# Layer 2 of a graph network's edge pipeline: features on partitions with 256 edges streaming, in place of edges on partitions

## The chip, the cores and the metric

The kernel runs on one core of a Trainium2 chip, as one program that computes the whole layer. The metric is the device time of one execution in microseconds (us), smaller being better. Durations inside an execution come from the hardware profiler. In what follows PE is TensorE (its matmuls; PEld are its weight loads), ACT is ScalarE, DVE is VectorE, POOL is GpSimd and SP is SyncE; a q behind a name (ACTq, SPq) is that engine's own instruction queue, where it issues DMAs and waits.

## The reference

There are 12500 nodes with 64 features each, and 200000 edges, sorted by their target `dst`. Each edge has 64 features of its own and a distance. With `ssp(v) = softplus(v) - log 2`, the reference computes

```python
nodes    = x[[src, dst]]                         # 128 numbers per edge
gates    = ssp(edge @ We1 + be1) @ We2 + be2     # 64 per edge
gates    = gates * (1 - sigmoid(5 * (distance - 3.5)))
h        = ssp(nodes @ Wn1 + bn1) @ Wn2 + bn2    # 64 per edge
message_sum = zeros.at[dst].add(h * gates)       # summed into the target node
new      = x + ssp(message_sum @ Ws1 + bs1) @ Ws2 + bs2
out      = layernorm(x + new)
```

All of it is float32.

## The kernel before

**Preparation.** The first 75 us load constants and compute a table, one row per node, of what a target node adds to the first layer. The additive constant of softplus is moved into the biases; each bias row is split into three bf16 pieces, so that a matmul of three rows can add it.

**The loop over edges.** The edges are taken in 391 groups of 512 (four lanes `k` of 128). Step `i` of the loop works on several groups at once: it loads for `i + 5`, gathers for `i + 14`, does the first layer of group `i + 1`, the second layer of group `i` and the sum into nodes of an earlier group. The order on every engine is the order in which the program writes the instructions.

- `gather` (L231): POOL issues an indirect DMA per lane, 128 rows of x by `src`. 47 of the 1564 lanes are fetched row by row instead, by plain DMAs on the queues of SP and ACT (`fetch`, L257: seven a step on SP, nine on ACT, with `read_rows`, L245, reading their addresses from a list). 1516 gathers are left for POOL. There are 19 buffers of gathered rows.
- `load` (L278, L286): SP brings the edges' features and the table's rows that the group's targets need.
- `transposes` (L307, or L304 for a lane fetched row by row): four transposes turn the gathered rows, with a one-hot of the target's place in a window of 42 nodes beside them, to features on partitions. They wait for the loads, the gathers and the one-hots of the group. `xcopy` (L314) on ACT copies the result to SBUF.
- First layer, with features on partitions: `layer1_bias` (L319), `layer1_edge` (L324) and `layer1_node` (L330) put 768 columns into PSUM tile `z` (two banks). `exps` (L341) and `logs` (L344) on ACT and `softplus` (L349) on DVE make `s` of them.
- Second layer, with edges on partitions: the activations are the stationary operand and the weights stream. `layer2_bias` (L354) adds both biases by a matmul of three rows, `layer2_edge` (L361) and `layer2_node` (L366) bring gates and h of the four lanes into one bank, tile `gh`, in two and four matmuls. On DVE `hcut` (L375) multiplies h by the cutoff and `message` (L379) multiplies that by the gates.
- `scatter` (L383): matmuls of the message with the one-hots sum the 512 messages into a window of 42 nodes, in the columns of the second bank of `z` that the first layer leaves free. `window` (L400) adds this to the sums in SBUF. It is done two groups behind (`i - 2`), and in the last steps, from `i = last - CLOSE` = 378 on, one group behind.

**Node blocks.** As soon as a block of 512 nodes has all its messages, its own two layers and its normalisation are cut into parts (`node_block`, L402 to L483) which are put into the following steps, after the step's own work: matmuls (L419, L447, L450), ACT work (L438, L439, L458, L466, L467), DVE work (the rest), a fetch and a store by SP. There are 25 blocks; the last is done when the loop is over. After the loop the last two groups are written out by hand.

A matmul of float32 is shown as two records, a transpose as one.

Of the kernel before, what the change touches and what calls it, by code (L numbers as in the profile page):

```python
# [57 lines left out]
P = 128  # L58
# [65 lines left out]
def gnn_resnorm_kernel(ctx: ExitStack, tc: tile.TileContext, a: dict, out: bass.AP, E: int):  # L124
# [56 lines left out]
    ones3 = const.tile([PIECES, HE], BF16, name="ones3")  # L181
    be3 = const.tile([PIECES, 2, D], BF16, name="be3")
    row3 = const.tile([PIECES, 2, K, D], BF16, name="row3")
    rs3 = const.tile([PIECES, K, D], BF16, name="rs3")
    wns = const.tile([DW, REST, 2, 2 * D], F32, name="wns")

# [100 lines left out]
                wns[D:DW, g % REST, h, :].bitcast(U8),  # L287
                table_bytes[:, bass.ds(bases[g][h], 8 * D * W)].rearrange("o (w f) -> (o w) f", w=W))), old)

    xTs, zs, us, ss, ghs, hs, msgs, scs = ({} for _ in range(8))  # L290

    def onehot(g):
        last = nc.vector.tensor_tensor(xgs[g][:, :, D:DW], iota, rel[:, g, :].to_broadcast([P, K, W]), OP.is_equal)  # L293
# [69 lines left out]
    def layer2_node(g):  # L363
        for h in range(2):
            for t in range(2):
                nc.tensor.matmul(ghs[g][:, 1, 2 * t + h, :], ss[g][:, 1 + h, t, :], wn2, start=False,  # L366
                                 stop=h == 1 and t == 1, skip_group_check=True)

    def layer2(g):
        layer2_edge(g)  # L370
        layer2_node(g)

    def hcut(g):
        hs[g] = work.tile([P, K, D], F32, name="h")
# [6 lines left out]
    def scatter(g, sc):  # L381
        for t in range(2):
            ins = nc.tensor.matmul(sc, msgs[g][:, 2 * t : 2 * t + 2, :].rearrange("p h f -> p (h f)"),  # L383
                                   xgs[g][:, 2 * t : 2 * t + 2, D:DW], start=t == 0, stop=t == 1, skip_group_check=True)
        note(("scatter", g), ins)
        scs[g] = sc
# [103 lines left out]
    with tc.manual_schedule():  # L490
# [4 lines left out]
        with tc.tile_pool(name="prep", bufs=1) as prep:  # L495
# [81 lines left out]
                    nc.vector.tensor_sub(rest, rest, pieces[:, q, :])  # L577
            nc.scalar.dma_start(row_d.rearrange("(o q) f -> o q f", o=1), pieces)
            rows = prep.tile([PIECES, 4, D], BF16, name="rows")
            nc.scalar.dma_start(rows.rearrange("q i d -> q (i d)"), row_d)  # L580
            for i in range(3, PARTS):
                load_x(i)
# [3 lines left out]
            for i in range(PARTS):  # L586
                for c in range(i * CP, (i + 1) * CP, CP // 2):
                    m = CP // 2
                    ps = z_tile().rearrange("p b (k f) -> p (b k) f", k=K)
                    for k in range(m):  # L590
                        nc.tensor.matmul(ps[:, k, :], xT[:, c + k, :], wnb, start=True, stop=True)
                    tb = prep.tile([P, m, 2 * D], F32, name="tb", bufs=6)
                    nc.scalar.copy(tb[:, :K, :], ps[:, :K, :])
                    nc.vector.tensor_copy(tb[:, K:, :], ps[:, K:m, :])
                    nc.sync.dma_start(by_node[:, c : c + m], tb)
                    nc.vector.memset(sums[:, c * P : WIDE if c + m == NCH else (c + m) * P], 0.0)
                if i == 1:
                    nc.vector.tensor_copy(base_i[:1], base_b[:1])
                    nc.vector.tensor_scalar(base_i[32:33], base_b[32:33], float(8 * D), None, OP.mult)
                    nc.vector.tensor_scalar(rows_i, rows_i, float(4 * D), None, OP.mult)  # L600
                    for k in range(2):
                        nc.vector.tensor_copy(be3[:, k, :], rows[:, 0, :])
                    for k in range(K):
                        nc.vector.tensor_copy(row3[:, :, k, :], rows[:, 1:3, :])
                        nc.vector.tensor_copy(rs3[:, k, :], rows[:, 3, :])
                if i == 2:
                    nc.scalar.activation(dist, dist, AF.Sigmoid, bias=steep, scale=-5.0)
                    nc.scalar.preload_act_table_set("natural_log_exp_and_others")
                    nc.vector.tensor_copy(rel, dst_i)
                    for t in range(2):  # L610
                        r = rel[:, :, 2 * t : 2 * t + 2]
                        nc.vector.tensor_sub(r, r, base_b[:, :NH].rearrange("p (g h) -> p g h", h=2))


        with tc.tile_pool(name="finish", bufs=1) as finish:
            blocks = list(zip(node_blocks(N), block_steps(N, NG)))
            last = NG - 1
            parts, begun, complete, rest = {}, None, 0, []

            def at(f, g, *more):  # L620
                if 0 <= g < NG:
                    f(g, *more)

            def behind_by(i):
                close = last - CLOSE
                return [g for g in ([i - 2] if i <= close else []) + ([i - 1] if i >= close else []) if g >= 0]

            for g in range(LOADS - 1):
                load(g)
            for g in range(2):  # L630
                onehot(g)
            for i in range(-1, last - 1):
                now = parts.pop(i, [])
                early = [part for part in now if part.tensor]
                at(load, i + LOADS)
                read_rows(i, 0, ROWS[0])
                fetch(i, 0, ROWS[0])
                if i >= 0:
                    at(gather, i + AHEAD)
                transposes(i + 1, ("load", i + 1), ("gather", i + 1), ("onehot", i + 1))  # L640
                xcopy(i + 1)
                read_rows(i, 1, ROWS[1])
                fetch(i, 1, ROWS[1] - 6)
                layer1_bias(i + 1)
                at(layer2_bias, i)
                for n, g in enumerate(behind_by(i)):
                    scatter(g, zs[i + 1][:, 1, HE + 2 * n * W : HE + 2 * (n + 1) * W])
                layer1_edge(i + 1)
                layer1_node(i + 1)
                exps(i + 1)  # L650
                fetch(i, 1, 3)
                logs(i + 1)
                fetch(i, 1, 3)
                for g in behind_by(i):
                    window(g)
                at(layer2, i)
                for part in early:
                    part.tensor(tx_tile())
                at(hcut, i)
                at(message, i)  # L660
                softplus(i + 1)
                for part in early:
                    part.others()
                at(onehot, i + 3)
                for part in now:
                    if not part.tensor:
                        part.others()
                complete = i
                if blocks and complete >= blocks[0][1] - PREPARE and not begun:
                    begun = node_block(*blocks[0][0], finish)  # L670
                    begun.pop(0).others()
                if blocks and complete >= blocks[0][1]:
                    steps = next(steps for steps in BLOCK_STEPS if i + steps[-1] < last - 1)
                    for n, part in zip(steps, begun):
                        parts.setdefault(i + n, []).append(part)
                    rest = begun[len(steps) :]
                    blocks.pop(0)
                    begun = None
            assert len(blocks) == 1 and begun and not parts


            begun.pop(2).others()
            transposes(last, ("load", last), ("gather", last), ("onehot", last))
            xcopy(last)
            layer1_bias(last)
            layer2_bias(last - 1)
            scatter(last - 2, zs[last][:, 1, HE : HE + 2 * W])
            layer1_edge(last)
            layer1_node(last)
            for some in (edge, node):  # L690
                exps(last, some)
                logs(last, some)
            square, variance, root, scale, store = (part.others for part in rest)
            square()
            window(last - 2)
            for g in range(last - 1, last + 1):
                window_bases(g)
            layer2(last - 1)
            layer2_bias(last)
            softplus(last, edge)  # L700
            layer2_edge(last)
            softplus(last, node)
            layer2_node(last)
            hcut(last - 1)
            message(last - 1)
            scatter(last - 1, tx_tile()[:, : 2 * W])
            variance()
            root()
            hcut(last)
            message(last)  # L710
            scatter(last, tx_tile()[:, : 2 * W])
            window(last - 1)
            window(last)
            hidden, clamp = begun.pop(0)
            hidden(gh_tile())
            scale()
            clamp()
            store()
            for part in begun:
                node_part(part)  # L720
# [152 lines left out]
```

## Time and profile before

| | us |
|---|---|
| median of 10 runs (1935.36 to 1939.39) | 1937.62 |
| the profiled execution, its own time | 1937.49 |
| its span, first to last instruction | 1935.6 |
| POOL busy (1516 gathers) | 1441.2 |
| PE busy | 1781.5 |
| ACT busy | 963.3 |
| DVE busy | 1053.1 |
| granted TensorE clock, mean | 0.972 |

Busy time is the sum of the instructions' durations with overlaps counted once. The ends of matmuls are modelled, so that distances between starts say more of PE than durations do. Groups of instructions are listed by line, engine and tile as `busy, mean ns of one | idle time of the engine just before them`, with what ended that idle time. In the order of time, a row has its start, its duration, engine, line and operation, how many instructions were merged into it, and in brackets the idle time before it. The waits list who waited for whom: total us, times, longest.

### The profile page before, as it was taken

The page shows a single profiled execution, that of the slowest core. Times are in us where ns is not written, and L with a number is a line of the kernel's source. Part 1 is how long each engine was busy: PE and PEld are TensorE (multiplying, and loading weights), DVE is VectorE, ACT ScalarE, POOL GpSimd, SP SyncE. Part 2 cuts the span into 40 slices and gives each one's busy share as a digit, 9 for nine tenths or more (in the row PEclk, how much of TensorE's full clock was granted, in tenths as well). Part 3 has the DMA queues.
Part 4 walks back from the last instruction along what each step waited for, and adds up shares of the span by engine and source line. Part 5 has one row for each costly group of instructions (what it writes and reads, how often), then busy time and mean ns, then how long its engine had stood idle before and what let it go on. Part 6 is the DMA issues. An engine that isn't in the chain of part 4 may idle for free.

```text
span 1935.6 us, 47845 instructions
## 1 busy us (share of the span) xinstructions
PE 1781.5 (92%) x11373; PEld 1463.4 (76%) x11373; DVE 1053.1 (54%) x2767; ACT 963.3 (50%) x1318; POOL 1441.4 (74%) x1520
## 2 busy tenths in 40 slices
PE   4899998999999999999999989999999999898997
PEld 4777777777777777777777777777777777787875
DVE  4455554554564554555555555555555555555565
ACT  1355554544554554545555555454555555555453
POOL 7777777777777777777777777777777777777773
PEclk9999999999998999999999999999999999999898
DMA  8422222222222222222222222222222222222220
GB/s 247 132 70 66 66 65 72 65 67 66 73 65 68 67 71 70 66 70 65 72 70 69 71 68 70 74 69 71 67 73 74 70 71 69 70 73 70 66 73 25
DMA packets 150911, 143.53 MB, mean 74 GB/s; under 512 B 51887, under 2 KB 98395, under 8 KB 150626
## 3 DMA queue, kind: packets, MB, share of 16 engines
q1 hardware_dynamic: 94090, 88.26, 15.7%
q0 software_dynamic: 48512, 49.77, 11.4%
q10 hardware_dynamic: 8024, 2.37, 0.6%
q8 instruction: 97, 1.59, 0.3%
q14 instruction: 188, 1.54, 0.3%
HBM read 130.59 MB, written 9.63 MB: 72 GB/s over the span
## 4 chain that ended last, share of the span: by engine, by line
PE 48%; ACTq 16%; issue 9%; SPq 9%; DMA 7%; ACT 6%; DVE 3%; POOL 2%; DVEq 0%; POOLq 0%
ACTq L257 13%; PE z L330 10%; PE gh L366 7%; PE z L383 7%; PE tx L307 6%; PE z L324 5%; PE gh L361 4%; SPq L257 4%; ACT xT L314 3%; DMA xg<-in_x,src_i 3%; PE gh L354 2%; DMA wns<-table 2%; PE z L319 2%; ACTq L245 2%; SPq L286 2%
## 5 line engine op out<-in xcount | busy, mean ns | idle before, releaser
L231 POOL DMA_INDIRECT xg<-in_x,src_i x1516 | 1441.2, 951 | 465.1 <-issue 346.9
L341 ACT ACTIVATE u<-z 128x768 f32<-128x768 f32 x392 | 317.0, 809 | 691.9 <-PE z L330 651.1
L400 DVE TENSOR_TENSOR sums<-sums,z 64x42 f32 x778 | 152.8, 196 | 771.9 <-ACT u L341 740.9
L330 PE MATMUL z<-xT,wns 106*128 106x256 f32 x1564 | 428.5, 398 | 8.0 <-ACT xT L314 7.2
L344 ACT ACTIVATE u<-u,one 128x768 f32<-128x768 f32 x392 | 366.0, 934 | 70.2 <-ACT u L341 66.1
L366 PE MATMUL gh<-consts,s 128*128 128x64 f32 x3128 | 399.0, 271 | 0.0
L366 PEld LDWEIGHTS gh<-consts,s 128*128 128x128 f32 x3128 | 389.1, 196 | 0.0
L349 DVE SCALAR_TENSOR_TENSOR s<-u,z 128x768 f32<-128x768 f32 x392 | 369.6, 943 | 12.5 <-ACT u L344 9.9
L330 PEld LDWEIGHTS z<-xT,wns 106*128 106x128 f32 x1564 | 299.7, 197 | 77.2 <-ACT xT L314 32.7
L307 PE MATMUL tx<-consts,xg 128*106 128x128 f32 x1517 | 237.0, 276 | 95.1 <-DMA wns<-table 33.0
L383 PEld LDWEIGHTS z<-xg,msg 128*128 128x128 f32 x1556 | 205.9, 193 | 125.8 <-issue 122.5
L314 ACT COPY xT<-tx 106x512 f32<-106x512 f32 x391 | 227.7, 582 | 132.2 <-PE tx L307 114.2
L383 PE MATMUL z<-xg,msg 128*128 128x84 f32 x1556 | 266.2, 294 | 0.7 <-DVE msg L379 0.2
L361 PEld LDWEIGHTS gh<-consts,s 128*128 128x128 f32 x1564 | 246.6, 199 | 24.6 <-DVE s L349 2.0
L324 PE MATMUL z<-eT,consts 128*128 128x256 f32 x782 | 255.5, 409 | 0.0
L307 PEld LDWEIGHTS tx<-consts,xg 128*106 128x106 f32 x1517 | 168.8, 139 | 112.3 <-issue 52.3
L361 PE MATMUL gh<-consts,s 128*128 128x128 f32 x1564 | 246.9, 281 | 1.7 <-DVE s L349 1.7
L375 DVE TENSOR_TENSOR h<-gh,cut 128x256 f32<-128x256 f32 x391 | 166.0, 425 | 31.4 <-PE gh L366 17.4
L379 DVE TENSOR_TENSOR msg<-gh,h 128x256 f32<-128x256 f32 x391 | 166.0, 424 | 13.4
L354 PE MATMUL gh<-row,ones 3*128 3x512 bf16 x391 | 147.6, 378 | 0.0
L293 DVE TENSOR_TENSOR xg<-consts,rel 128x168 f32<-128x168 f32 x391 | 128.4, 329 | 0.0
L324 PEld LDWEIGHTS z<-eT,consts 128*128 128x128 f32 x782 | 121.7, 197 | 0.9 <-issue 0.9
(93 smaller groups left out, 587.5 us busy)
## 6 DMA issues: line engine op xcount, KB each, us to landing
xr<-in_x ACTq DMA_DIRECT2D x3328, 0.2 KB
eT<-in_eT SPq DMA_DIRECT2D x195, 256.0 KB
xr<-in_x SPq DMA_DIRECT2D x2688, 0.2 KB
xg<-in_x,src_i POOLq DMA_INDIRECT x1516
wns<-table SPq DMA_DIRECT2D x782, 21.0 KB
table<-tb SPq DMA_DIRECT2D x14, 448.0 KB
sums<-in_xT SPq DMA_DIRECT2D x7, 455.0 KB
y<-in_x SPq DMA_DIRECT2D x24, 128.0 KB
```

Of the source, the lines that this page charges most:

```text
L231: note(("gather", g), nc.gpsimd.indirect_dma_start(out=xg[:, k, :D], out_offset=None, in_=x, in_offset=bass.IndirectOffsetOnAxis(ap=src_i[ ...
L257: ins = queues[queue].dma_start(row_tiles[n, "in"][r : r + 1, :D].bitcast(U8), x_bytes[:, bass.ds(row_at[queue].pop(0), 4 * D)])
L307: ins = nc.tensor.transpose(tx[:, k, :], xgs[g][:, k, :DW], ident)
L314: note(("xcopy", g), nc.scalar.copy(xT, xTs[g]))
L324: nc.tensor.matmul(zs[g][:, 0, :HE], we1.rearrange("a h d -> a (h d)"), eTs[g], start=False, stop=True, skip_group_check=True)
L330: nc.tensor.matmul(zn, wns[:, g % REST, h, :], xTs[g][:, h], start=True, stop=True, skip_group_check=True)
L341: nc.scalar.activation(us[g][:, part], z_of(g)[:, part], AF.Exp)
L344: nc.scalar.activation(us[g][:, part], us[g][:, part], AF.Ln, bias=one)
L349: nc.vector.scalar_tensor_tensor(ss[g].rearrange("p i t e -> p (i t e)")[:, part], us[g][:, part], BIG, z_of(g)[:, part], OP.min, OP.max)
L361: nc.tensor.matmul(v[:, 0, t], ss[g][:, 0, t, :], we2, start=False, stop=False, skip_group_check=True)
L366: nc.tensor.matmul(ghs[g][:, 1, 2 * t + h, :], ss[g][:, 1 + h, t, :], wn2, start=False, stop=h == 1 and t == 1, skip_group_check=True)
L383: ins = nc.tensor.matmul(sc, msgs[g][:, 2 * t : 2 * t + 2, :].rearrange("p h f -> p (h f)"), xgs[g][:, 2 * t : 2 * t + 2, D:DW], start=t = ...
```

## The change

The second layer of a group is turned round within the loop. `features` streams the 256 edge columns of each half through stationary weights: one matmul with the two copies of We2 on the diagonal gives the gates of both halves on 128 partitions, and two with Wn2 give h, one half on partitions 0 to 63 and the other on 64 to 127. `gates` copies the gates to SBUF on ACT and adds their bias, which is now one number per partition (`sides2`). `products` adds the bias of h and multiplies by the gates, in one instruction on DVE. `turn` brings the 256 messages back to edges on partitions with two transposes on PE, into the columns of `gh` where the gates stood, one step later. `weigh` multiplies by the cutoff and writes `msg`. `layer2_bias`, `layer2`, `hcut` and `message` are no longer called in the loop; the last two groups, behind the loop, keep the old form.

The order within a step changes with it. For `2 <= i <= 378` (`far_on`) the group scattered is still `i - 2`, in the old place; `turn(i - 1)` stands behind the first layer's matmuls, and `products` behind `softplus`. From 378 on (`near`), `turn(i - 1)` stands ahead of `layer1_node`, `products` ahead of `softplus`, and `scatter(i - 1)` behind `exps` and `logs`.

```diff
+    sides2 = const.tile([P, 2], F32, name="sides2")
...
+    def features(g):
+
+        gh = gh_tile()
+        gT, hT = gh[:, :HE], gh[:, HE:]
+        nc.tensor.matmul(gT, we2.rearrange("a h d -> a (h d)"), ss[g][:, 0].rearrange("p t e -> p (t e)"),
+                         start=True, stop=True, skip_group_check=True)
+        for h in range(2):
+            nc.tensor.matmul(hT[h * D : (h + 1) * D], wn2, ss[g][:, 1 + h].rearrange("p t e -> p (t e)"),
+                             start=True, stop=True, skip_group_check=True)
+        ghs[g] = gh
+
+    def gates(g):
+        turns[g] = work.tile([P, 2, P], F32, name="mT")
+        nc.scalar.activation(turns[g].rearrange("p t e -> p (t e)"), ghs[g][:, :HE], AF.Identity,
+                             bias=sides2[:, 0:1])
+
+    def products(g):
+        mT = turns[g].rearrange("p t e -> p (t e)")
+        nc.vector.scalar_tensor_tensor(mT, ghs[g][:, HE:], sides2[:, 1:2], mT, OP.add, OP.mult)
+
+    def turn(g):
+        for t in range(2):
+            nc.tensor.transpose(ghs[g][:, t * P : (t + 1) * P], turns[g][:, t], ident)
+
+    def weigh(g):
+        msgs[g] = work.tile([P, K, D], F32, name="msg", bufs=3)
+        nc.vector.tensor_mul(msgs[g], ghs[g][:, :HE].rearrange("p (k d) -> p k d", k=K),
+                             cut[:, g, :].to_broadcast([P, K, D]))
...
                     for k in range(2):
                         nc.vector.tensor_copy(be3[:, k, :], rows[:, 0, :])
+                        nc.vector.tensor_copy(rows2[:, :, k, :], rows[:, 1:3, :])
+                    ps = gh_tile()
+                    for q in range(2):
+                        nc.tensor.matmul(ps[:, q : q + 1], rows2[:, q].rearrange("q k d -> q (k d)"), ones3[:, :1],
+                                         start=True, stop=True)
+                    nc.vector.tensor_copy(sides2, ps[:, :2])
...
                 layer1_bias(i + 1)
-                at(layer2_bias, i)
-                for n, g in enumerate(behind_by(i)):
-                    scatter(g, zs[i + 1][:, 1, HE + 2 * n * W : HE + 2 * (n + 1) * W])
+                far_on, near = i <= last - CLOSE and i >= 2, i >= last - CLOSE
+                if far_on:
+                    scatter(i - 2, zs[i + 1][:, 1, HE : HE + 2 * W])
                 layer1_edge(i + 1)
+                if near:
+                    turn(i - 1)
                 layer1_node(i + 1)
                 exps(i + 1)
                 fetch(i, 1, 3)
                 logs(i + 1)
                 fetch(i, 1, 3)
-                for g in behind_by(i):
-                    window(g)
-                at(layer2, i)
+                if far_on:
+                    window(i - 2)
+                if i >= 1 and not near:
+                    turn(i - 1)
+                if i >= 1:
+                    weigh(i - 1)
+                if near:
+                    scatter(i - 1, zs[i + 1][:, 1, HE + 2 * W : HE + 4 * W])
+                    window(i - 1)
+                at(features, i)
+                at(gates, i)
                 for part in early:
                     part.tensor(tx_tile())
-                at(hcut, i)
-                at(message, i)
+                if near:
+                    products(i)
                 softplus(i + 1)
+                if not near:
+                    at(products, i)
                 for part in early:
                     part.others()
...
             layer1_bias(last)
+            layer1_edge(last)
+            turn(last - 2)
+            layer1_node(last)
+            weigh(last - 2)
             layer2_bias(last - 1)
             scatter(last - 2, zs[last][:, 1, HE : HE + 2 * W])
-            layer1_edge(last)
-            layer1_node(last)
```

More of the change, by code (lines that the diff above doesn't have):

```diff
@@ L288, in load @@
                 table_bytes[:, bass.ds(bases[g][h], 8 * D * W)].rearrange("o (w f) -> (o w) f", w=W))), old)
-    xTs, zs, us, ss, ghs, hs, msgs, scs = ({} for _ in range(8))
+    xTs, zs, us, ss, ghs, hs, msgs, scs, turns = ({} for _ in range(9))
     def onehot(g):
@@ L579, in gnn_resnorm_kernel @@
             rows = prep.tile([PIECES, 4, D], BF16, name="rows")
+            rows2 = prep.tile([PIECES, 2, 2, D], BF16, name="rows2")
             nc.scalar.dma_start(rows.rearrange("q i d -> q (i d)"), row_d)
@@ L622, in at @@
                     f(g, *more)
-            def behind_by(i):
-                close = last - CLOSE
-                return [g for g in ([i - 2] if i <= close else []) + ([i - 1] if i >= close else []) if g >= 0]
             for g in range(LOADS - 1):
```

## The prediction

> **What bounds the kernel now.** I read the page's groups first, then the waits, then the order of time in three places: the middle, a steady stretch, and the end.
>
> The first group, and then POOL's waits (total, times, longest, in us):
>
> ```profile
> L231 POOL DMA_INDIRECT xg<-in_x,src_i x1516 | 1441.2, 951 | 465.1 <-issue 346.9
> ```
>
> ```profile
> POOL xg L231 <- issue: 346.9, 1137, 0.3
> POOL xg L231 <- DMA xg<-in_x,src_i: 47.3, 155, 0.3
> ```
>
> POOL gathers rows of x, 1516 times 0.95 us, and the longest idle stretch in front of a gather is 0.3 us whoever is named: it never waits. The first gather begins at 3.26 us, and 1516 x (0.951 + 0.30) = 1897 us later, by the trace at 1906.7, the last one ends. The span is 1935.6, so all that follows the last gather takes 28.9 us. The change leaves the number of gathers alone, so 1906.7 stands unless POOL is made to wait. Nothing here can be won but in those 28.9 us, and a loss comes in where the other engines fall behind POOL.
>
> How near are they to that? A step's first transposes (L307) are its mark on PE. Four transposes make a step; counted through, step 0 begins at 74.97, step 210 at 1036.60, step 379 at 1856.86, the last one, 390, at 1909.95. Up to about step 215 the loop works off what POOL gathered during the preparation: 961.6 us / 210 = 4.58 us a step. From there on it is (1856.86 - 1036.60) / 169 = 4.85 us, POOL's pace (1516 / 391 gathers x 1.25 us), and steps begin 2 to 3 us after their last gather ended. Undisturbed, a step takes less:
>
> ```profile
> 118.29 0.60 PE L307 MATMUL tx<-consts,xg 128*106 128x128 f32 x4
> 118.82 0.28 PE L319 MATMUL z<-ones,be 3*128 3x256 bf16 x1
> 118.94 0.38 PE L354 MATMUL gh<-row,ones 3*128 3x512 bf16 x1
> 119.25 0.68 PE L383 MATMUL z<-xg,msg 128*128 128x84 f32 x4
> 119.76 0.63 PE L324 MATMUL z<-eT,consts 128*128 128x256 f32 x2
> 120.23 1.03 PE L330 MATMUL z<-xT,wns 106*128 106x256 f32 x4
> 121.09 0.61 PE L361 MATMUL gh<-consts,s 128*128 128x128 f32 x4
> 121.54 1.00 PE L366 MATMUL gh<-consts,s 128*128 128x64 f32 x8
> 122.38 0.60 PE L307 MATMUL tx<-consts,xg 128*106 128x128 f32 x4
> ```
>
> The distances of the starts are what each group costs PE: 0.53, 0.12, 0.31, 0.51, 0.47, 0.86, 0.45, 0.84, in all 4.09 us. So PE has 0.5 us to spare a step before step 215 (SP's queue, which issues seven row fetches and the loads, sets 4.58) and 0.76 after it.
>
> The last view is of DVE's waits, with the order of time near the end beside it:
>
> ```profile
> DVE sums L400 <- ACT u L341: 740.9, 376, 5.7
> ```
>
> ```profile
> 1889.25 0.81 ACT L341 ACTIVATE u<-z 128x768 f32<-128x768 f32 x1 [1.97 <-PE z L330]
> 1890.09 0.41 DVE L400 TENSOR_TENSOR sums<-sums,z 64x42 f32 x2 [1.51 <-ACT u L341]
> 1890.53 0.42 DVE L375 TENSOR_TENSOR h<-gh,cut 128x256 f32<-128x256 f32 x1
> 1890.99 0.42 DVE L379 TENSOR_TENSOR msg<-gh,h 128x256 f32<-128x256 f32 x1
> 1891.34 0.94 DVE L349 SCALAR_TENSOR_TENSOR s<-u,z 128x768 f32<-128x768 f32 x1
> ```
>
> The window add reads columns of z that the exponential does not touch, and still begins 0.03 us after the exponential's end, 376 times. Instructions of two engines on one bank of z are kept apart in program order. This decides below.
>
> **The far steps, i = 2 to 377.** PE loses L354 (0.31), L361 (0.45) and L366 (0.84): 1.60. It gains the gates' matmul, as one of L324, 0.47; the two of h, as those of L330, 0.86 if one follows the other; two transposes, half of L307's 0.53, 0.27; and 0.08, since L319 must now wait out the same turn to full height that L354 had behind it. 1.68: PE's step would be 4.17. Unknown is what it costs that h's matmuls use 64 columns each: nothing in the trace writes partitions 64 to 127 alone. From below, they overlap: 0.43 for the two, 3.74 for the step. From above I take the dearest turn between shapes that PE shows (0.1 us, L307 to L319 and L354 to L383) on each of three sides: 4.47. I take 4.25.
>
> The Trainium skill, page TensorEngine Tiling (Array Packing), Key Properties, has both: a change of tiling mode drains TensorE, and different tiles work in parallel. By the parallel half a step would be 3.74, by the drain nearer to 4.47; no run here shows either.
>
> ScalarE gets the gates' activation, 128x256 from PSUM: 0.38 as L341 without a bias, 0.51 as L344 with one; I take 0.5. Queued behind it are the next copy of xT, the row list and nine row fetches, which fill ACT's queue in an undisturbed step (copy at 208.37, next at 212.45). The block's square (L458) stands in this place already: at 547.34 it takes 0.42, and the queue's list load starts 0.04 later, while it still runs. So the gates cost the queue 0.04 and the copy 0.5, and the next exponential comes about 0.1 later: 4.2 for ACT. DVE changes two products of 0.42 for two of 0.42 to 0.48. The turn waits for the products of the step before, with features and then the gates behind it: from the exponential's start the logarithm ends 1.9 us later, softplus 2.9, products 3.45, and PE comes to the turn about 3.9 later. All of it stays under 4.58, so far steps cost nothing; POOL and SP hide them. In the preparation, four small copies, two matmuls and a copy (about 1.5 us) move step 0, which POOL's lead of 67 us covers.
>
> **The near steps, i = 378 to 388.** Here the message of step i - 1 is turned, weighed and scattered within step i, and the scatter now stands behind the exponential in the program, in the same bank of z. So the steps form one chain, with no work of another step to fill it: exponential 0.81 (L341), hop 0.06, scatter 0.51, features 0.47 + 0.86 and 0.22 until they are in PSUM (L330's issue to L341's start), gates 0.5, hop 0.06, products 0.45 (between L442's 0.42 and L434's 0.48), hop 0.06, turn 0.3, L330 0.86 behind it in PE's order and 0.22 to land, then the next exponential. 5.4 us a step, where POOL gives 4.85. 11 x 5.4 = 59.4.
>
> Node-block work lies on top. DVE's own row between products and scatter (softplus 0.94, one-hot 0.33, weigh 0.42, gaps) is 1.8 us beside 2.4 of turn, L330 and exponential: 0.55 spare. The window holds 7.7 us of block work on DVE, bunched at steps 378 and 385 (two clamps of 0.95, two scales of 1.1, centers of 0.83): about 4.5 come out. PE's four block stages there (3.0 us of L419, L447 and L450) have about 0.1 spare each: 2.4. ScalarE's two pairs L438 and L439 (0.93 each) delay the copy that L330 needs: 1.4. Step 378 also has the old window add ahead of its weigh: 0.9. Together 9.2, so 68.6 us from step 379 to 390, where the profile before has 53.1: +15.5.
>
> Were two engines free to use one bank on different columns, the scatter would not wait for the exponential, and the longest circle would be gates, products, softplus, one-hot, weigh, scatter, features: 5.0 a step, and the sum 4.4 us less. The Trainium skill, page PSUM — Partial Sum Buffer, section PSUM bank collisions raise a hardware error, asks for the wait (two engines are to be kept apart by bank, even reads from reads), and the 376 waits above agree; by the page it is +15.5, by columns alone +11.
>
> **Behind step 390.** L354 and the scatter no longer stand before L330, which gains 0.6; the weigh of step 388 comes behind softplus and center, which costs layer 2 of step 389 1.2 us, with 2 us of waiting for softplus (L361's 1.74) behind it to take that up. 0.
>
> **Sum.** 1935.6 + 15.5 = 1951.1 for the span, and 1.9 outside it (the profiled execution's 1937.49 - 1935.6): 1953. That execution lies 0.1 under the median of 1937.62. With h's matmuls overlapping (-0.43 a near step) and gates at 0.38: 1947; with three turns of 0.1: 1956, and if the block work comes out in full (13.9 instead of 9.2), 1961.
>
> **Rivals.** (1) PE becomes the bound of every step. Up to step 378 the loop may average (1852.77 - 74.97) / 378 = 4.70 us. Block matmuls (24 times 1.5 us on PE, 0.1 a step), every eighth step's second row list on ACT (0.6, so 0.08) and late loads leave about 4.5 for PE's floor. It decides from 4.5 on, that is if the column halves cost over 0.3 us a step; each 0.1 beyond costs 378 x 0.1 = 38 us. At 4.56: 23 + 3 more in the near steps, 1979. Against it: the turns seen cost 0.1 at most. (2) Nothing moves: the near steps' chain is shorter than I think, say because exponential and scatter overlap and block work hides, and 4.9 keeps up with POOL: 1938. Against it: the bank wait is in the trace 376 times. (3) Faster, the other side: the loop ends as it does and only the close changes. The one mechanism is L330 of step 390, which is 0.6 earlier, and a lighter PE, which lets step 390 begin when its last gather lands, 1.5 us after 1906.7 (the least distance in this trace), and not at 1909.95. 0.6 + 1.7 = 2.3 us: 1935. Needs near steps under 4.2; under 0.2% even then, and over it only with more that I don't see.
>
> **How the numbers follow.** About 0.2% (3.9 us) is what a measurement of this kernel can tell from no change. Forecast (far steps hidden, near steps bare, 1942 to 1963): 0.68. Rival 1: 0.18, of which a good half stays under 1979. Rival 2: 0.11, rival 3: 0.03, of which I give a faster result over 0.2% 0.02. The range 1938 to 1979 leaves out about 0.09 above and 0.09 below. Faster 0.02, same 0.11, slower 0.87.
>
> **What would show it.** Right: POOL's gathers still run 0.30 apart to about 1907; PE's undisturbed step lies between 3.8 and 4.5; the mean of the steps to 378 is as before; steps 379 to 390 take 64 to 72 us, with scatters there starting just behind the end of an exponential, and PE waiting for products in front of the turns. Wrong: gathers that wait for buffers, a PE step of over 4.5 throughout (rival 1), or steps 379 to 390 still in 54 us (rival 2).

## The result: slower by 11 us, all of it in the last steps

The changed kernel takes 1947.9 us (median of 8 runs, 1946.6 to 1951.1), the kernel before 1936.7: ratio 1.0059, 95% interval 1.0050 to 1.0068. A second comparison gave 1951.3 against 1937.7, 1.0065 (1.0052 to 1.0079). The forecast was slower, 1953. The profiled execution of the first comparison took 1954.5 us (span 1952.7), some 6 us above the median, which is taken up below.

POOL first, from the page's groups and from the waits (total, times, longest):

```profile
L232 POOL DMA_INDIRECT xg<-in_x,src_i x1516 | 1441.0, 951 | 465.3 <-issue 329.0
```

```profile
POOL xg L232 <- issue: 329.0, 1078, 0.3
POOL xg L232 <- DMA xg<-in_x,src_i: 49.6, 162, 0.4
```

The gathers run as before and the last one ends at 1906.8 us, as before (in the profile of the second comparison, whose longest wait in front of a gather is 0.7 us, at 1909.8). So POOL was not made to wait, and the time is lost in what follows it. Counting the first transposes of the steps (now L308) through gives the place:

| first transposes | before | after | after, second comparison |
|---|---|---|---|
| step 20 to 378, mean of a step | 4.727 | 4.709 | 4.713 |
| step 379 | 1856.86 | 1856.00 | 1859.36 |
| step 390 | 1909.95 | 1927.25 | 1926.17 |
| step 379 to 390 | 53.1 | 71.3 | 66.8 |
| from step 390 to the end | 25.7 | 25.5 | 25.9 |

The far steps and the end are as they were; the eleven near steps hold the loss. In both profiles of the changed kernel a part of this stretch ran at half the TensorE clock, a different part in each. Steps 379 to 386 at full clock in the first (45.9 us) and 387 to 389 at full clock in the second (17.6) make 63.4 us for the whole stretch, 10.3 more than before; the half clock is taken up below. One near step, not stretched by node-block work, in the order of time (start, duration, engine, line, operation; in brackets the idle time before it and what ended it):

```profile
1888.01 0.81 ACT L342 ACTIVATE u<-z 128x768 f32<-128x768 f32 x1 [1.24 <-PE z L331]
...
1888.88 0.68 PE L413 MATMUL z<-xg,msg 128*128 128x84 f32 x4 [0.90 <-ACT u L342]
...
1889.39 0.64 PE L378 MATMUL gh<-s,consts 128*128 128x256 f32 x2
...
1889.95 0.65 PE L381 MATMUL gh<-s,consts 128*64 128x256 f32 x4
...
1890.65 0.47 ACT L387 ACTIVATE mT<-gh,sides 128x256 f32<-128x256 f32 x1 [0.86 <-PE gh L381]
...
1891.16 0.48 DVE L392 SCALAR_TENSOR_TENSOR mT<-gh,sides,mT 128x256 f32<-128x256 f32 x1 [1.09 <-ACT mT L387]
...
1891.86 0.38 PE L396 MATMUL gh<-consts,mT 128*128 128x128 f32 x2
...
1892.08 1.03 PE L331 MATMUL z<-xT,wns 106*128 106x256 f32 x4
...
1893.14 0.81 ACT L342 ACTIVATE u<-z 128x768 f32<-128x768 f32 x1 [1.34 <-PE z L331]
```

This is the circle of the prediction, row for row: the scatter (L413) waits 0.90 us for the exponential and starts 0.06 behind its end, features (L378, L381) queue behind it, and so to the next exponential, 5.13 us later, where POOL's pace is one step in 4.85.

### The profile page after: what moved, and what is told of

Read it like the earlier page. It is cut to its first block, busy times and chain, and to the rows that moved or that the text cites. A ratio compares the mean times of both kernels' runs of the same rounds, so it can differ in the third digit from the quotient of the medians.

```text
span 1952.7 us, 44803 instructions
## 1 busy us (share of the span) xinstructions
PE 1733.7 (89%) x9430; PEld 1154.4 (59%) x9430; DVE 1074.6 (55%) x2770; ACT 1116.6 (57%) x1707; POOL 1441.2 (74%) x1520
## 4 chain that ended last, share of the span: by engine, by line
PE 46%; ACTq 11%; DMA 10%; ACT 9%; issue 9%; SPq 7%; DVE 4%; POOL 4%; DVEq 0%; POOLq 0%
PE z L331 13%; ACTq L258 9%; PE z L413 7%; PE tx L308 6%; DMA xg<-in_x,src_i 6%; PE z L325 5%; PE gh L381 4%; POOL xg L232 4%; PE gh L378 3%; SPq L258 3%; ACT u L342 3%; DMA wns<-table 2%; ACTq L246 2%; PE z L320 2%; ACT mT L387 2%
## 5 line engine op out<-in xcount | busy, mean ns | idle before, releaser
L331 PE MATMUL z<-xT,wns 106*128 106x256 f32 x1564 | 434.4, 401 | 28.6 <-ACT xT L315 25.3
L331 PEld LDWEIGHTS z<-xT,wns 106*128 106x128 f32 x1564 | 285.2, 194 | 136.5 <-ACT xT L315 103.1
L308 PE MATMUL tx<-consts,xg 128*106 128x128 f32 x1517 | 246.9, 283 | 120.9 <-DMA xg<-in_x,src_i 36.5
L308 PEld LDWEIGHTS tx<-consts,xg 128*106 128x106 f32 x1517 | 156.4, 132 | 264.7 <-DVE msg L400 91.8
L413 PE MATMUL z<-xg,msg 128*128 128x84 f32 x1556 | 264.6, 292 | 20.6 <-DVE msg L400 11.0
L381 PE MATMUL gh<-s,consts 128*64 128x256 f32 x1556 | 256.0, 408 | 0.0
L325 PE MATMUL z<-eT,consts 128*128 128x256 f32 x782 | 253.7, 407 | 0.0
L413 PEld LDWEIGHTS z<-xg,msg 128*128 128x128 f32 x1556 | 204.4, 191 | 73.6 <-DVE msg L400 14.9
L378 PE MATMUL gh<-s,consts 128*128 128x256 f32 x778 | 236.3, 386 | 0.0
L387 ACT ACTIVATE mT<-gh,sides 128x256 f32<-128x256 f32 x389 | 184.0, 473 | 52.9 <-PE gh L381 15.4
L392 DVE SCALAR_TENSOR_TENSOR mT<-gh,sides,mT 128x256 f32<-128x256 f32 x389 | 185.9, 478 | 14.4 <-ACT mT L387 14.4
L400 DVE TENSOR_TENSOR msg<-gh,cut 128x256 f32<-128x256 f32 x389 | 165.1, 424 | 16.9 <-PE gh L396 4.9
L381 PEld LDWEIGHTS gh<-s,consts 128*64 128x64 f32 x1556 | 77.6, 136 | 131.1 <-issue 131.1
L396 PE MATMUL gh<-consts,mT 128*128 128x128 f32 x778 | 152.1, 277 | 0.0
L396 PEld LDWEIGHTS gh<-consts,mT 128*128 128x128 f32 x778 | 112.2, 144 | 41.1 <-issue 2.2
```

The source lines that it names most:

```text
L308: ins = nc.tensor.transpose(tx[:, k, :], xgs[g][:, k, :DW], ident)
L325: nc.tensor.matmul(zs[g][:, 0, :HE], we1.rearrange("a h d -> a (h d)"), eTs[g], start=False, stop=True, skip_group_check=True)
L331: nc.tensor.matmul(zn, wns[:, g % REST, h, :], xTs[g][:, h], start=True, stop=True, skip_group_check=True)
L378: nc.tensor.matmul(gT, we2.rearrange("a h d -> a (h d)"), ss[g][:, 0].rearrange("p t e -> p (t e)"), start=True, stop=True, skip_group_che ...
L381: nc.tensor.matmul(hT[h * D : (h + 1) * D], wn2, ss[g][:, 1 + h].rearrange("p t e -> p (t e)"), start=True, stop=True, skip_group_check=True)
L396: nc.tensor.transpose(ghs[g][:, t * P : (t + 1) * P], turns[g][:, t], ident)
```

## The experiments

Theory: far steps are free, and near steps are long because features stands on PE behind a scatter that waits for the exponential on the same bank of z. Rivals: the far steps or the preparation cost something; or the near steps are long through the mere number of new operations in series.

Every ratio is against the kernel before in the same sitting, that is, a set of runs made together on one chip. In some sittings that kernel took 1937 us, in others 2635 to 2637, and in the latter POOL was not the bound; they are read separately.

### Halves and remedies, where the kernel before takes 2637 us

The new far steps with the old near steps, and the reverse:

```diff
 # far new, near old: in the near steps
-turn(i - 1); weigh(i - 1); scatter(i - 1, ...); features(i); gates(i); products(i)
+layer2_bias(i); scatter(i - 1, ...); layer2(i); hcut(i); message(i)
 # far old, near new: the same exchange for i < last - CLOSE
```

> Steps up to 377 as in the changed kernel (features, gates, products, turn, weigh), steps 378 to 388 and the two behind them as in the kernel before. Theory (all 11 us are lost in the near steps, the far steps are hidden behind POOL's gathers): 1936.7 us, between 1935 and 1939; 53 us from the first transpose of step 379 to that of step 390. Rival 1 (the far steps' longer work delays the gathers' consumers as well): 1940 to 1948, with step 378 reached later than 1852.8 us or POOL's last gather later than 1906.8. Rival 2 (the preparation's longer part or the end costs it): 1940 to 1948 with step 378 at the same place.

> Steps up to 377 as in the kernel before, steps 378 to 388 and the two behind them as in the changed kernel. Theory: the whole loss is here, 1947.9 us, between 1945 and 1951, with 64 to 72 us from the first transpose of step 379 to that of step 390. Rivals 1 and 2 (the loss is in the far steps, or in the preparation): 1937 to 1942. The two runs' losses should add to the 11 us of the change.

Two remedies for the near steps, one by order, one by place:

```diff
 # features first
-if near: scatter(i - 1, ...); window(i - 1)
 at(features, i)
 at(gates, i)
+if near: scatter(i - 1, ...); window(i - 1)
 # own bank
-scatter(i - 1, zs[i + 1][:, 1, HE + 2 * W : HE + 4 * W])
+scatter(i - 1, ghs[i - 1][:, HE : HE + 2 * W])
```

> The changed kernel, but in the near steps TensorE runs features(i), and the gates are issued, ahead of scatter(i-1) and its window; the scatter still goes into the bank that exps(i+1) reads, and so still waits for it. Theory (the near step is long because features stands behind a scatter that waits for exp: exp .81, hop .06, scatter .51 lie in the chain): without them the chain of a step is features .47+.59+.22, gates .5, products .45, turn .3, node matmul .86+.22, hop, exp .81 no longer in the circle with features: some 4.2 to 4.5 us a step, below the 4.85 that the gathers take: 1937 to 1941. Rival 3 (the near step is long through the sum of its new operations: gates, products, turn and weigh in series, whatever the scatter waits for): 1944 to 1949, steps still at 5.1.

> The changed kernel, but in the near steps the scatter of step i-1 goes into the second half of gh(i-1), which products has emptied by then, instead of the bank of z that exps(i+1) reads, so it does not wait for exps. The order on TensorE is unchanged. Theory (it is the wait on exps): the circle is then products .45, weigh .42, scatter .51, features 1.3, gates .5, with hops of .06 to .2, and the other one turn .3, node 1.1, exp .81, log and softplus, some 4.2 to 4.6 us a step: 1937 to 1941. Rival 3 (the number of operations in series, not the bank): 1944 to 1949, steps still at 5.1, with the scatter waiting for weigh instead of exps.

Two of them were run once more and met the same condition again.

> Steps up to 377 as in the changed kernel, steps 378 to 388 and the two behind them as in the kernel before, once more (the first run of it was on a chip on which the kernel before itself took 2637 us and POOL no longer bounds it). Where the kernel before takes 1937 us: theory (all 11 us are lost in the near steps) 1936.7, between 1935 and 1939, and 53 us from the first transpose of step 379 to that of step 390; the far steps or the preparation as the cause: 1940 to 1948. Where the kernel before takes 2637 us again: 0.978 of it, as in the first run.

> The changed kernel with the near scatter in the second half of gh(i-1) instead of the bank of z that exps(i+1) reads, once more. Where the kernel before takes 1937 us: theory (the wait on exps makes the near step 5.1 us) 1937 to 1941, near steps of 4.2 to 4.6 us where undisturbed; rival 3 (gates, products, turn and weigh in series, whatever the scatter waits for): 1944 to 1949, steps still at 5.1 with the scatter waiting for weigh. On the chip of the first run, the undisturbed near steps were at 3.92 to 4.6 us between stretches in which every engine stood still, which speaks for the theory.

Measured:

| kernel | us | ratio (95%) | step 379 to 390 |
|---|---|---|---|
| far new, near old | 2577.7 | 0.978 (0.974 to 0.983) | 51.9 |
| the same again | 2568.6 | 0.975 (0.970 to 0.980) | 53.5 |
| far old, near new | 2656.1 | 1.009 (1.005 to 1.013) | 63.3 |
| features first | 2578.5 | 0.977 (0.973 to 0.982) | 52.7 |
| own bank | 2574.9 | 0.976 (0.972 to 0.981) | 59.0 |
| own bank again | 2580.8 | 0.978 (0.973 to 0.982) | 57.2 |

The times expected in the first four are for a condition that these runs did not meet. For the condition that they met, only the repetition of far new, near old had a number: 0.978 expected, 0.975 measured. The last column can still be read: in these executions POOL's last gather for step 390 had ended some 68 to 85 us before the step began, so the stretch shows the chain of the near steps with no gather to wait for. Only the new near steps as they were changed take 63 us; with features first they take no more than the old ones, with a bank of its own for the scatter they take something in between.

What makes these sittings slow was not settled. The waits show POOL, which never waited before, waiting up to 70 us for room (far old, near new; total, times, longest):

```profile
POOL xg L232 <- PE z L413: 365.2, 148, 70.1
```

and SP needs 3.7 us in the median for seven row fetches that took 2.2 in the profile before. One of the longer ones (first row that kernel, second row the kernel before):

```profile
1923.03 4.11 SPq L258 DMA_DIRECT2D xr<-in_x  x7
```

```profile
1364.61 2.20 SPq L257 DMA_DIRECT2D xr<-in_x  x7
```

All kernels with new far steps (44,788 to 44,893 instructions) came to 0.973 to 0.978 there, that with old ones (47,760) to 1.009. That fits a late supply of instructions, but nothing here shows it. The granted clock was lower there as well (0.82 to 0.89 in the mean of an execution, against 0.96 to 0.99), and whether that is a cause or a consequence is open. The changed kernel itself was not run in such a sitting.

### The change again, and without row fetches

```diff
-slots = slots_by_rows(NG)
+slots = []          # by_rows is empty: POOL gathers everything
```

> The changed kernel as it is, beside the kernel before. Where the kernel before takes 1937 us: 1947.9. On chips on which the kernel before takes 2637 us (two calls so far) the two halves of the change have been timed by themselves: new far steps with old near steps 0.975 to 0.978, old far steps with new near steps 1.0086. If the halves add, the whole change is faster there, 0.983 to 0.987 of before, 2592 to 2603 us; if the new near steps cost nothing beside new far steps, 0.977; if the far steps' gain is lost again through the near ones, 1.0.

> The kernel before without the rows that SP and ACT read: POOL gathers all 1562 places that are not padding, 46 more than the 1516 (the result is the same). SP and ACT lose 6016 DMA issues with a register move each, some 12,000 of the 47,845 instructions of the profile. By POOL alone: 46 x 1.251 us = 57.5 us more than 1937, 1994. Theory for the chips on which before takes 2637 us (every engine's own stream of instructions arrives late there: SP's register moves of 0.029 us take 0.70 us some 470 times, while each packet of instructions takes as long as before): fewer instructions free POOL to bound again, 1990 to 2150 us, 0.75 to 0.82 of before. Rival (those chips are slow at something else: TensorE's granted clock of 0.84, memory, or the gathers): the gathers get more and nothing else gets faster, 2600 to 2700 us. Where the kernel before takes 1937 us, 1990 to 1998.

> The changed kernel without the rows that SP and ACT read, as in g2. If POOL bounds every step at 4 x 1.251 = 5.0 us: theory (far steps hidden; near steps of 5.1 us, so hardly longer than the gathers' 5.0, but node-block work beside them and two of them behind the last gather): 2 to 10 us above g2. Rival 1 (the far steps cost something, though hidden from the profile): 15 us or more above g2, reached before step 378. Rival (the time of these chips follows the number of instructions, which the change lowers by 3,042): 20 us or more below g2.

In this sitting the kernel before took 1937.7 again. The changed kernel: 1951.3, told above. The kernel before without row fetches: 1993.0 (1.0283, 1.0269 to 1.0297), against 1994 by POOL's arithmetic (the trace has 1563 gathers, 47 more and not 46). That confirms POOL as the bound; the theory on the sittings of 2637 us stayed untested by it. The changed kernel without row fetches: 2008.6 (1.0353, 1.0339 to 1.0368), 15.6 us above, where I expected 2 to 10. Step 379 began at 1913.5 us, 0.6 later than at 1912.9 in the kernel before without row fetches, and the stretch from there to step 390 took 68.8 instead of 53.6: +15.2 of the +15.6. So the far steps are free at 5.0 us a step, too. My expectation compared a bare near step, 5.13, with 5.0; it named the node-block work and gave it too little, and that is there whatever POOL's pace. And it left out half clock: from 1965.0 to 1978.7 us this profile has the clock at 0.5, and the last three near steps take 6.55, 10.00 and 6.31 us where the second comparison's profile has 6.06, 6.43 and 5.08 at full clock. Some 5 us of the +15.2 are that, and +10 is left, the upper end of what I expected.

### The two remedies, where the kernel before takes 1937 us

> The changed kernel with features(i) and gates ahead of scatter(i-1) in the near steps; the scatter still goes into the bank that exps(i+1) reads and still waits for it. Where the kernel before takes 1937 us: theory (the near step is long because features stands on TensorE behind a scatter that waits for exp) 1936 to 1941, 53 to 56 us from step 379 to step 390 instead of 66.8 to 71.3. In its first run, on a chip of 2637 us, this stretch was 52.7 us, with undisturbed steps of 3.98, where old far steps with new near steps took 63.3. Rival 3 (the sum of the new operations in series): 1946 to 1952, the stretch at 64 or more. Where before takes 2637 us again: 0.977 of it.

> The changed kernel with the near scatter in the second half of gh(i-1), so that it waits for weigh alone; the order on TensorE is unchanged. Where the kernel before takes 1937 us: theory (it is the wait on exps, and order matters only through it) 1937 to 1943, 54 to 60 us from step 379 to step 390; its two runs on chips of 2637 us had undisturbed steps of 3.92 to 4.6 and 5.4 in the steps with node-block work. Rival 3: 1946 to 1952, the stretch at 64 or more. If both of these kernels come to the time of before, the bank and the order are two ways out of one chain; if only the first does, the order alone decides. Where before takes 2637 us again: 0.977 of it.

| kernel | us | ratio (95%) | step 379 to 390 |
|---|---|---|---|
| features first | 1938.2 | 1.0004 (0.9995 to 1.0013) | 54.1 |
| own bank | 1940.9 | 1.0019 (1.0010 to 1.0028) | 59.8 |

Both came out as the theory said, against 1946 to 1952 for the rival. Features first takes the whole loss away, with the same operations in the same number, the scatter still in the same bank:

```profile
1887.02 0.81 ACT L342 ACTIVATE u<-z 128x768 f32<-128x768 f32 x1 [1.34 <-PE z L331]
...
1887.35 0.65 PE L381 MATMUL gh<-s,consts 128*64 128x256 f32 x4
...
1887.86 0.93 ACT L345 ACTIVATE u<-u,one 128x768 f32<-128x768 f32 x1
...
1887.93 0.68 PE L413 MATMUL z<-xg,msg 128*128 128x84 f32 x4
```

PE works on features while the exponential runs, and comes to the scatter when the bank is free: the scatter has no idle time in front. With a bank of its own the scatter runs beside the exponential, in the same order as in the changed kernel:

```profile
1888.98 0.81 ACT L342 ACTIVATE u<-z 128x768 f32<-128x768 f32 x1 [1.22 <-PE z L331]
...
1889.00 0.68 PE L413 MATMUL gh<-xg,msg 128*128 128x84 f32 x4
...
1889.51 0.63 PE L378 MATMUL gh<-s,consts 128*128 128x256 f32 x2
```

It starts 0.02 behind the exponential's start, released by the weigh. This step takes 4.45 us (transposes at 1886.20 and 1890.65), its neighbours 3.92 and 4.59; in the changed kernel the same three take 5.13, 5.08 and 5.13. But 3.5 us of loss stay: features still stands behind weigh, which DVE does after softplus, one-hot and any node-block work. Twice the scatter waits 1.82 us for the weigh, and half clock follows for 6.8 and 3.4 us; in the repetition above, at full clock and with no gather to wait for, the stretch takes 57.2 us and not 59.8. With features first no wait of PE in the stretch reaches 1.2 us, and the clock is full throughout. So the wait on the bank was the larger part, and the order decides all of it. Features first comes to 1.0004 with the new far steps in place, which also shows that those steps are free in the time and not only in the trace.

### The dose

```diff
-CLOSE = 12
+CLOSE = 2           # step 388 alone is near
```

> The changed kernel with CLOSE = 2 instead of 12: step 388 alone is near, and steps 378 to 387 stay in the order of the far ones, with scatter two steps behind. A test by dose. Where the kernel before takes 1937 us: theory (each near step costs what its chain of 5.1 us and the node-block work beside it lie above the gathers' 4.85) a tenth of the loss is left, 1937 to 1941, and 53 to 57 us from step 379 to step 390. Rival (the loss is in the last two steps and their end, where the gates and the turn come one after the other, and not in the steps ahead of them): 1946 to 1952. Where before takes 2637 us: 0.975 to 0.980 of it.

It fell into a sitting of 2635 us: 2566.4, 0.9732 (0.9684 to 0.9781), a little below the range given for that. The stretch from step 379 to 390 takes 54.9 us, within the 53 to 57 of the theory. Since all kernels with new far steps come to about the same there, its time says nothing on the dose where POOL bounds; the trace alone supports it.

No version ran faster than the kernel before where POOL bounds: by features first the change costs nothing and brings nothing there.

## Why the prediction was right, and where its sizes were off

**What bounds the kernel, and the far steps: right.** The gathers stand 0.30 apart to the end, and the mean of the far steps stays within 0.02 us. PE's undisturbed step in the changed kernel:

```profile
525.34 0.60 PE L308 MATMUL tx<-consts,xg 128*106 128x128 f32 x4
525.87 0.28 PE L320 MATMUL z<-ones,be 3*128 3x256 bf16 x1
526.08 0.68 PE L413 MATMUL z<-xg,msg 128*128 128x84 f32 x4
526.60 0.63 PE L325 MATMUL z<-eT,consts 128*128 128x256 f32 x2
527.07 1.03 PE L331 MATMUL z<-xT,wns 106*128 106x256 f32 x4
527.93 0.38 PE L396 MATMUL gh<-consts,mT 128*128 128x128 f32 x2
528.15 0.60 PE L378 MATMUL gh<-s,consts 128*128 128x256 f32 x2
528.68 0.65 PE L381 MATMUL gh<-s,consts 128*64 128x256 f32 x4
529.26 0.65 PE L308 MATMUL tx<-consts,xg 128*106 128x128 f32 x4
```

3.92 us, where I took 4.25 between 3.74 and 4.47, and the kernel before has 4.09. (A step up to 210 still takes 4.56 us in the first profile and 4.58 in the second, 4.58 before, so PE did not set that pace.) The term that was off is the pair of 64-column matmuls of h (L381): 0.58 us to the next start, not 0.86. The two halves run side by side, as two groups of the changed kernel's profile show:

```profile
L381 PE MATMUL gh<-s,consts 128*64 128x256 f32 x1556 | 256.0, 408 | 0.0
L325 PE MATMUL z<-eT,consts 128*128 128x256 f32 x782 | 253.7, 407 | 0.0
```

L381 has twice as many records as L325, as long in the mean, and keeps PE busy no longer. Record by record, in the step above, the first ones of the two halves start within 0.01 us of each other (528.68), and so do the second ones (528.95). That alone would make 0.43. The rest is in the turns between shapes: 0.31 us pass from the last record of L378 to the first of L381, and 0.31 again from the last of L381 to L308, where the two records of L378 start 0.22 apart; 0.05 more lie between the two pairs of L381. The gates' matmul L378 so costs 0.53, not 0.47. The Trainium skill, TensorEngine Tiling (Array Packing), Key Properties, expects both a drain at a change of mode and parallel tiles: these rows agree with both, and a turn into or out of the 64-column shape costs about 0.1 us. Both my bounds were thus partly right, the overlap of the lower and the turns of the upper. Rival 1 (PE as the bound from 4.5 on) falls with that.

**The near circle: right in its links, 0.25 too long.** By the rows shown under the result, beside the terms of the prediction:

| link, start to start | predicted | measured |
|---|---|---|
| exponential, hop | 0.87 | 0.87 |
| scatter | 0.51 | 0.51 |
| gates' matmul L378 | 0.47 | 0.56 |
| h's pair L381 and landing | 1.08 | 0.70 |
| gates, hop | 0.56 | 0.51 |
| products, hop | 0.51 | 0.70 |
| turn | 0.30 | 0.22 |
| L331 and landing | 1.08 | 1.06 |
| sum | 5.38 | 5.13 |

The largest miss is again L381, by -0.38. Products to turn went the other way, +0.19: before the transposes PE loads weights (PEld), and this load, too, waits for the products, which I had not counted.

```profile
1891.70 0.30 PEld L396 LDWEIGHTS gh<-consts,mT 128*128 128x128 f32 x2
```

It begins 0.06 behind the end of the products, and the first transpose another 0.16 later. Over eleven steps the circle is 2.8 us shorter than predicted.

**Node-block work: 9.2 predicted, 7.0 measured**, as what the stretch at full clock holds beyond the bare circle: 63.4 - 11 x 5.13. The bunch that I named is plain to see in step 387: two clamps, the root and a scale, mean and center stand on DVE in front of the weigh, and the scatter waits 2.07 us for it:

```profile
1903.36 1.03 PE L331 MATMUL z<-xT,wns 106*128 106x256 f32 x4
1906.45 0.65 PE L413 MATMUL z<-xg,msg 128*128 128x84 f32 x4 [2.07 <-DVE msg L400]
```

**Behind step 390 and the preparation: right.** 25.5 and 25.9 us against 25.7; step 0 began 1.30 us later in the first profile for my 1.5 (6.0 later in the second), and by step 379 nothing of it was left in the first.

**The sum: too high, by the circle and the block work.** At full clock the stretch is 63.4 us against 53.1, +10.3 for +15.5 predicted. Half clock, which the prediction did not have, added 7.8 us in the profile of the first comparison and 3.4 in that of the second. The measured losses, +11.2 and +13.6, lie somewhat above +10.3; their intervals (9.7 to 13.2 us, and 10.1 to 15.3) overlap. How much of them is half clock is not shown, since only the profiled executions have the clock step by step. That both profiled stretches (71.3 and 66.8) lie within the 64 to 72 us that I gave as a sign is in part luck: without half clock it is 63.4.

**A number that fits for the wrong reason.** The alternative without a wait on the bank gave +11, which is what the first comparison measured. The trace decides against it: the scatter starts 0.06 behind the exponential's end. And where the wait really is away (own bank), the loss is 3.5 us: that alternative's circle was sized at 5.0, and the step shown takes 4.45, shorter by L381 and by one-hot and weigh following closely on softplus. The Trainium skill, PSUM — Partial Sum Buffer, section PSUM bank collisions raise a hardware error, asks for two engines to be kept apart by bank; 0.06 behind with one bank and 0.02 behind the start with two agree with it.

Rival 2 (nothing moves) did not come true for the change as it stands; it is what features first measured. Rival 3's end was not reached by any version.

**What I did not predict** is in the last stretch of the first comparison's profile. Windows of the trace; behind the length stand the five engines' busy times (PE, PEld, DVE, ACT, POOL), then the granted clock:

```profile
1856.00:1907.00 51.00, 40.26 (x219) 26.20 (x220) 26.78 (x76) 26.09 (x41) 38.59 (x41) 1.00 0.21 53
1907.00:1928.00 21.00, 19.20 (x62) 11.38 (x61) 6.00 (x17) 6.78 (x11) 0.00 (x0) 0.51 0.04 9
```

From just behind the wait of 2.07 us PE ran at half clock for 21 us: L381 took 1.12 instead of 0.65, L331 1.92 instead of 1.03, and the last two near steps 9.99 and 8.62 us. The second comparison's profile has 1.00 in the same place, the last three steps (387 to 389) taking 6.06, 6.43 and 5.08 us:

```profile
1910.00:1931.00 21.00, 16.78 (x97) 11.05 (x96) 10.86 (x31) 10.05 (x17) 0.00 (x0) 1.00 0.06 15
```

The first took 25.4 us for these three, so half clock cost it 7.8 us. The second has its half clock earlier, 6.8 us of it from 1864.65 on, behind another scatter that waited:

```profile
1864.65 1.12 PE L413 MATMUL z<-xg,msg 128*128 128x84 f32 x4 [1.91 <-ACT u L345]
1866.63 1.12 PE L381 MATMUL gh<-s,consts 128*64 128x256 f32 x4
```

Its steps 379 and 380 take 10.19 and 5.94 us where the first profile, at full clock there, has 7.49 and 5.27: 3.4 us more. Whether half clock is why the first profiled execution lies above the median is not shown; its mean clock, 0.981, is within the 0.980 to 0.986 of the other executions.

## What to carry to other kernels

Where an engine takes its work in order, an instruction that waits costs what is queued behind it, so the first remedy is to let independent work pass ahead of it: here it took away the whole loss, more than removing the wait itself. Cost a serial stretch by its circle, from start to start, and add the work that shares its engines; do not compare the bare circle with the pace of the bound. And a change that lightens an engine which is not the bound (here PE, 92% busy, with an undisturbed step of 3.92 us for 4.09) brings nothing until the bound moves; in sittings where POOL was not the bound, the new far steps with the old near ones were worth 2.2 to 2.5%.

## What the hardware showed that I had not expected

- **Half clock after a short wait, sometimes.** The profiles of the versions with new near steps have fourteen waits of PE of 1.81 to 2.07 us in front of a near scatter. Nine were followed within 1.6 us by half clock, for 3.4 to 20.5 us, and five were not; of two waits of 1.91 us in the second comparison's profile, the first was and the second was not. The Trainium skill, TensorE: Matmul & The Clock Gate, Part 1, tells of an activity window of about 3.4 us that runs freely, so that the same wait can or cannot fall into it. The lengths of the half clock, 3.41, 6.83, 13.65 and 20.48 us, are multiples of 3.41 and agree with that; they don't prove it. All fourteen waits are shorter than that window; what decides whether one, two, four or six windows follow, or none, is open. It makes a chain of waits near the end cost more than its waits.
- **Two 64-column matmuls in a row** into different halves of the partitions ran side by side and cost 0.58 us, where two whole ones of the same stream cost 0.86; some 0.1 us at each change of shape is what kept it from 0.43.
- **The same kernel at 1937 and at 2637 us.** In three of the sittings the kernels that were also run in the others took 634 to 700 us longer, POOL waited for room and SP's row fetches took 1.7 times as long in the median. The record has chip 0 in a sitting of each kind. Kernels with the new far steps were ahead of the kernel before there; the cause stays open.
